# A convolution and attention kernel in fp32: a smaller GpSimd lag while keys are made, and three changes in the closing stage

## The chip, the cores and the metric

The kernel runs on one core of a Trainium2 chip. The metric is the device time of one execution in microseconds (us); lower is better. Engines are named as the profile names them: PE is TensorE (PEld its weight loads), DVE is VectorE, ACT is ScalarE, POOL is GpSimd, SP is SyncE, which issues nearly all DMAs here.

## The reference

The input is four images of 512 channels by 64 x 64 pixels, in fp32. Layer 0 is self-attention over the 4096 pixels of each image with 128 inner channels; layer 1 is an involution (a 7 x 7 filter whose weights are computed for each pixel and for each of 8 groups of 16 channels). Both add their input as a residual. Cut to what matters:

```
q, k, v = wq @ x + bq, wk @ x + bk, wv @ x + bv          # 128 x 4096 per image
attn    = softmax(q^T k)                                 # 4096 x 4096
x       = wo @ (v attn^T) + bo + x                       # 512 x 4096

o = relu(s1 * (W1 @ x) + b1)                             # 128 x 4096
w = Ws @ relu(sr * (Wr @ o) + br) + bs                   # 49 weights per pixel and group
i = sum over the 49 taps of w[tap] * o shifted by tap    # zero padding of 3
x = s3 * (W3 @ i) + b3 + x
```

## The kernel before

An image's 4096 pixels are cut into 8 chunks of 512 pixels (the last chunk of the last image into two halves). For each image there are two stages on PE.

**Making keys** (`keys_values`). The chunks are loaded in the order 2 to 7, 1, 0. For each, PE makes the keys `pk` (four matmuls of 512 columns) and the values `pv` (sixteen of 128 columns); ACT copies both to SBUF.

**Attention** (`attention`). For each chunk of queries PE alternates between scores `pss` (128 keys by 512 queries) and output `po`; ACT takes the exponential into `pt`, and DVE adds the tiles up in `pacc` for the denominator. When a chunk is done, a generator `finish_block` normalises it (`blocks`, `pl`, `rls`, `spread`, `on`), multiplies by Wo (`pwo`, four tiles, each evicted by DVE with the residual, line L513), makes `o1` by W1 (`p1`; the profile calls it `p`), turns it to pixels on partitions (`pp`, `o1t`), writes it to a padded image `pix` in DRAM, and makes the input of the per-pixel weights (`pr`, `red`).

**The involution** (`involution`) runs beside both stages in units of 4 rows of the image, 16 units an image, two units a chunk. Pixels lie on the partitions. `ring` holds 12 rows of the padded image, each with its 7 horizontal shifts, loaded by `pump` from `pix`. `weights` makes `pw`, the 392 weights of each pixel, on PE. A unit is a list of `ops`, 14 to 21 of them: an op is one horizontal shift x and n vertical shifts (n = 4 or 3, or parts of these when the ring wraps around). DVE multiplies the ring rows by the weights (L339), into `acc` for the first op and into one of four buffers `prod` for the others, and POOL adds the product to `acc` (L363). At the end of a unit POOL adds the four parts of `acc` together (L374), `turn_unit` turns the sum to channels on partitions (`pa`, `accT`), and `close_chunk` multiplies a chunk by W3 (`py`, four tiles, each evicted by DVE with scale and residual, L417) and issues the output DMA.

Everything is recorded in one order by a planner. `pe` is its estimate of PE's time, `free["dve"]` and `free["pool"]` its estimates of when the queues of DVE and POOL run empty. `chores` is called between PE's steps and takes one step of `finishing`, one of `closing`, and some of `taps` (the involution). An op of the involution is held back while these estimates are too far ahead of `pe`:

```
while not tail and (
    pe < max(begin, landed)
    or free["dve"] > pe + (4.5 if b == B - 1 else 3.5)
    or free["pool"] > pe + 7.5
):
    yield "wait"
```

When attention of the last image is done, `tail` is set and three queues are emptied in turn: `finishing`, `closing`, `taps`. In this closing stage, some 80 us, the products of odd ops are added by PE and not by POOL: a matmul with the identity `ident` as stationary operand and the product as moving operand adds them into the PSUM tile `accp` (two of the four rows side by side). At the end of such a unit ACT copies `accp` to `accs`, and `turn_unit` turns and adds the four parts of `acc` and the two of `accs` in one group of matmuls with `ident` moving.

`judge` looks whether all reciprocals of the denominators `rls` lie in a safe range (three DVE operations over 128 x 512), sums that over partitions by a small matmul `pn` and writes `verdict`, which decides at the very end whether a slower general path is run; with these inputs it is not.

PSUM tiles with the tag "mm" (`pq`, `pl`, `spread`, `pwo`, `p1`, `pp`, `pr`, `pa`, `py`, `pn`) share two buffers, in turn. All matmuls made by the helper `mm` have line L208.

Of the kernel before, what the change touches and what calls it, by code (L numbers as in the profile page):

```python
# [15 lines left out]
P = 128  # L16
# [53 lines left out]
ROW_US, X_US, PIX_US, LAND_US = 2.2, 3.8, 1.5, 3.0  # L70
HOP_US = 0.8
STEP_US = 1.0
PIECE = 3
TB = 32
WARM = 8
# [5 lines left out]
def fast_path(  # L81
# [65 lines left out]
    pe = 0.0  # L147
    due, seen = 0.0, 0.0
    free = {"dve": 0.0, "pool": 0.0, "dma": 0.0}
    tail = []  # L150
    reds, sums_c = {}, {}
    written = {}
    landing = {}
    low, load = 0, 0

    def until(us):
# [121 lines left out]
    def judge():  # L278
        ok = const.tile([P, B * N // TB], F32, name="ok")
        tc.keep_in_program_order(nc.vector.tensor_scalar(ok, rls, SAFE[0], None, ALU.is_ge))  # L280
        nc.vector.scalar_tensor_tensor(ok, rls, SAFE[1], ok, ALU.is_le, ALU.mult)
        okr = const.tile([P, 1], F32, name="okr")
        nc.vector.tensor_reduce(okr, ok, AX.X, ALU.min)
        pn = ps.tile([1, 1], F32, tag="mm", name="pn")
        nc.tensor.matmul(pn, lhsT=okr, rhs=ones[:, :1], start=True, stop=True)
        nc.vector.tensor_scalar(verdict, pn, P - 0.5, None, ALU.is_lt)


    def involution():
        nonlocal low, due  # L290
        while True:
            while not units:
                yield "none"
            b, u = units.pop(0)
            acc = work2.tile([P, NT, 4, P], F32, tag="acc", name=f"acc_{b}_{u}")
            yield from until(free["dve"] + 0.3)
            pw = early.pop((b, u), None) or weights(b, u)
            begin = pe + 0.5
            accp, ops = None, []
            base = b * STEP + u * UR  # L300
            for dy0, n in DYS:

                at = (base + dy0) % RING
                whole = at + n + NT < RING + 1
                pieces = [(dy0, n)] if whole else [(dy0, 2), (dy0 + 2, n - 2)]
                ops += [(x, dy, k) for x in range(K) for dy, k in pieces]
            for o, (x, dy, n) in enumerate(ops):
                if o and dy >= DYS[1][0] > ops[o - 1][1]:
                    low = base + UR
                    pump()  # L310
                    if tail and units:
                        early[units[0]] = weights(*units[0])
                rows = [(base + dy + t * 2) % RING for t in range(NT)]
                while base + dy + n + NT > load:
                    yield "wait"
                landed = max(landing[base + dy + i] for i in range(n + NT))
                while not tail and (
                    pe < max(begin, landed)
                    or free["dve"] > pe + (4.5 if b == B - 1 else 3.5)
                    or free["pool"] > pe + 7.5  # L320
                ):
                    yield "wait"
                free["pool"] = max(free["pool"], takes("dve", DVE_TAPS[0] + DVE_TAPS[1] * n))
                takes("pool", POOL_TAPS[0] + POOL_TAPS[1] * n)
                due -= n
                d0 = dy - DYS[dy >= DYS[1][0]][0]
                first = x == 0 and dy < DYS[1][0]
                prod, p0 = acc, d0
                if not first:
                    prod, p0 = prods.tile(  # L330
                        [P, NT, 4, P], F32, tag="prod", name=f"prod_{b}_{u}_{o}"
                    ), 0
                col = (x * K + dy) * G
                lines = ring[:, rows[0] : rows[0] + n, x, :]
                image = bass.AP(
                    tensor=lines.tensor, offset=lines.offset,
                    ap=[lines.ap[0], [(rows[1] - rows[0]) * K * P, NT], [K * P, n], [1, P]],
                )
                nc.vector.tensor_tensor(  # L339
                    prod[:, :, p0 : p0 + n, :].rearrange("p t d (g c) -> p t d g c", g=G),  # L340
                    image.rearrange("p t d (g c) -> p t d g c", g=G),
                    pw[:, :, col : col + n * G].unsqueeze(3)
                    .broadcast_to([P, NT, n * G, GC])
                    .rearrange("p t (d g) c -> p t d g c", d=n),
                    ALU.mult,
                )
                if first:
                    pass
                elif tail and o % 2 and (accp is not None or n > 1):

                    begin_sum = accp is None
                    if begin_sum:
                        accp = ps1.tile(
                            [P, NT, 2, P], F32, tag=("po", "acc")[u % 2], name=f"accp_{b}_{u}"
                        )
                    for d in range(0, n, 2):
                        k = min(2, n - d)
                        mm(
                            accp[:, :, :k, :], ident, prod[:, :, d : d + k, :],
                            begin_sum and d == 0, o + 2 >= len(ops) and d + 2 >= n,  # L360
                        )
                else:
                    nc.gpsimd.tensor_tensor(  # L363
                        acc[:, :, d0 : d0 + n, :], acc[:, :, d0 : d0 + n, :], prod[:, :, :n, :],
                        ALU.add,
                    )
                yield
            low = max(low, (b + 1) * STEP if u == NU - 1 else base + UR)
            pump()
            if (b, u) == (B - 1, NU - 1):  # L370
                judge()
            if accp is None:
                for n in (2, 1):
                    nc.gpsimd.tensor_tensor(  # L374
                        acc[:, :, :n, :], acc[:, :, :n, :], acc[:, :, n : 2 * n, :], ALU.add
                    )
            closing.append(turn_unit(b, u, acc, accp, takes("pool", POOL_OP * 1.5)))


    def turn_unit(b, u, acc, accp, done):  # L380
        c, k = divmod(u, 2)
        yield from until(done + 2.0)
        for _ in range(7 if tail else 0):
            yield
        last = (b, c) == (B - 1, NCH - 1)
        if last or k == 0:
            sums_c[b, c] = work1.tile([P, CH], F32, tag="accT", name=f"accT_{b}_{c}")
        pa = ps.tile([P, NT, P], F32, tag="mm", name=f"pa_{b}_{u}")
        if accp is None:
            for t in range(NT):  # L390
                nc.tensor.transpose(pa[:, t, :], acc[:, t, 0, :], ident)
            pe_us(0.25)
        else:

            accs = work1.tile([P, CH // P, P], F32, tag="o1t", name=f"accs_{b}_{u}")
            nc.scalar.copy(accs, accp.rearrange("p t d c -> p (t d) c"))
            for t in range(NT):
                parts = [acc[:, t, d, :] for d in range(4)] + [accs[:, 2 * t + d, :] for d in range(2)]
                for i, part in enumerate(parts):
                    mm(pa[:, t, :], part, ident, i == 0, i == len(parts) - 1)  # L400
        n = NT * P
        nc.scalar.copy(sums_c[b, c][:, k * n : (k + 1) * n], pa.rearrange("p t c -> p (t c)"))
        yield
        if last:
            closing.append(close_chunk(b, c, k * n, n, sums_c.pop((b, c))))
        elif k:
            closing.append(close_chunk(b, c, 0, CH, sums_c.pop((b, c))))


    def close_chunk(b, c, off, n, acc):  # L410
        xt = xs[b, c][:, :, off : off + n]
        yield
        for t in range(CT):
            py = ps.tile([P, CH], F32, tag="mm", name=f"py_{b}_{c}_{off}_{t}")[:, :n]
            mm(py, w_slice(O_W3, t), acc[:, off : off + n])
            takes("dve", DVE_OP * n / CH)
            nc.vector.scalar_tensor_tensor(  # L417
                xt[:, t, :], py, v1(V_S3 + t), xt[:, t, :], ALU.mult, ALU.add
            )
            if n < CH:  # L420
                nc.sync.dma_start(out_r[b, :, t, c * CH + off : c * CH + off + n], xt[:, t, :])
            for _ in range(2):
                yield
        takes("dma", X_US)
        if n == CH:
            nc.sync.dma_start(out_r[b, :, :, c * CH + off : c * CH + off + n], xt)
# [208 lines left out]

    taps = [involution()]
    for b in range(B):
        kv = keys_values(b)
        if b == 0:

            pb = ps.tile([P, CT], F32, tag="mm", name="pb")
# [412 lines left out]
```

## Time and profile before

| | |
|---|---|
| time, median of 3 runs | 2645.77 us (2645.48 to 2646.93) |
| the profiled execution | 2645.35 us, of which its span is 2643.6 us |
| matmuls on PE | 7478 recorded passes, busy 99% of the span |
| DVE, POOL, ACT | busy 70%, 69%, 33% of the span |
| stages of the span | keys of image 0 to about 128 us; keys of images 1, 2, 3 from about 620, 1265, 1910 us, each some 80 us; the closing stage from about 2560 us |

A busy share is an average over stages of different kinds, and PE's ends are modelled from a pipeline, so 99% does not say that PE is at its peak. Every fp32 matmul is recorded as two passes. A line such as `L339 DVE TENSOR_TENSOR prod<-ring,pw 128x768` gives source line, engine, operation, the tile written and those read, and the shape; brackets at its end give the engine's idle time before it and what ended it. Names are without numbers: `acc` is `acc_b_u` for every image and unit. Products and sums of a unit are counted in the order of its ops, from 0.

### The profile page before, as it was taken

The page shows a single profiled execution, that of the slowest core. Times are in us where ns is not written, and L with a number is a line of the kernel's source. Part 1 is how long each engine was busy: PE and PEld are TensorE (multiplying, and loading weights), DVE is VectorE, ACT ScalarE, POOL GpSimd, SP SyncE. Part 2 cuts the span into 40 slices and gives each one's busy share as a digit, 9 for nine tenths or more (in the row PEclk, how much of TensorE's full clock was granted, in tenths as well). Part 3 has the DMA queues.
Part 4 walks back from the last instruction along what each step waited for, and adds up shares of the span by engine and source line. Part 5 has one row for each costly group of instructions (what it writes and reads, how often), then busy time and mean ns, then how long its engine had stood idle before and what let it go on. Part 6 is the DMA issues. An engine that isn't in the chain of part 4 may idle for free.

```text
span 2643.6 us, 24069 instructions
## 1 busy us (share of the span) xinstructions
PE 2614.5 (99%) x7478; PEld 1254.9 (47%) x7478; DVE 1851.5 (70%) x2602; ACT 870.0 (33%) x1454; POOL 1821.4 (69%) x1197
## 2 busy tenths in 40 slices
PE   9999999999999999999999999999999999999998
PEld 7444444445544444444554444444464444444574
DVE  0437788776575778778566677878847667787887
ACT  1333333332333333333223333333323333333330
POOL 0007788788761788888784377878888467777875
PEclk9999999999999999999999999999999999999999
DMA  6032323325614233332450423333353423222343
GB/s 233 0 74 60 92 66 77 77 57 140 157 35 105 60 92 92 92 82 65 121 143 13 106 60 92 92 92 92 92 142 107 97 60 85 69 62 61 75 90 100
DMA packets 104730, 231.70 MB, mean 88 GB/s; under 512 B 5576, under 2 KB 24464, under 8 KB 104464
## 3 DMA queue, kind: packets, MB, share of 16 engines
q1 hardware_dynamic: 104160, 229.70, 35.2%
q8 instruction: 61, 1.00, 0.2%
q14 instruction: 77, 0.63, 0.1%
q10 hardware_dynamic: 432, 0.36, 0.0%
HBM read 187.28 MB, written 42.77 MB: 87 GB/s over the span
## 4 chain that ended last, share of the span: by engine, by line
PE 91%; POOL 4%; DMA 2%; DVE 2%; issue 1%; ACT 0%; SPq 0%; POOLq 0%; DVEq 0%; ACTq 0%
PE pss L208 32%; PE po L208 32%; POOL acc L363 4%; PE pq L208 4%; PE p L208 4%; PE py L208 4%; PE pwo L208 4%; PE pv L208 3%; PE pk L208 3%; DMA ring<-pix 2%; PE pw L208 2%; DVE prod L339 1%; PE pr L208 1%; PE pp L543 1%; PE accp L208 0%
## 5 line engine op out<-in xcount | busy, mean ns | idle before, releaser
L363 POOL TENSOR_TENSOR acc<-acc,prod 128x768 f32<-128x768 f32 (+3 forms) x1063 | 1699.6, 1619 | 797.5 <-DVE prod L339 694.7
L208 PE MATMUL pss<-q,k 128*128 128x512 f32 (+1 forms) x2112 | 1055.2, 584 | 2.3 <-ACT q L469 2.3
L208 PE MATMUL po<-pt,v 128*128 128x512 f32 (+1 forms) x2112 | 1047.0, 580 | 0.0
L596 ACT ACTIVATE pt<-pss 128x512 f32<-128x512 f32 x1024 | 611.2, 597 | 1219.0 <-PE pss L208 1198.7
L339 DVE TENSOR_TENSOR prod<-ring,pw 128x512 f32<-128x512 f32 (+3 forms) x1092 | 899.9, 849 | 147.6 <-POOL acc L363 93.4
L627 DVE TENSOR_TENSOR pacc<-pacc,pt 128x512 f32<-128x512 f32 x958 | 665.3, 695 | 415.6 <-ACT pt L596 405.9
L208 PEld LDWEIGHTS po<-pt,v 128*128 128x128 f32 x2112 | 398.6, 190 | 477.5 <-issue 458.7
L208 PEld LDWEIGHTS pss<-q,k 128*128 128x128 f32 x2112 | 389.3, 190 | 455.0 <-issue 436.3
L208 PE MATMUL py<-accT,wt 128*128 128x512 f32 (+1 forms) x264 | 133.0, 587 | 13.8 <-DVE x L513 12.7
L417 DVE SCALAR_TENSOR_TENSOR x<-py,vec,x 128x512 f32<-128x512 f32 (+1 forms) x132 | 96.4, 730 | 53.6 <-PE py L208 51.6
L208 PEld LDWEIGHTS pv<-wt,x 128*128 128x128 f32 x1024 | 123.3, 198 | 14.8 <-issue 14.8
L208 PE MATMUL pwo<-on,wt 128*128 128x512 f32 (+1 forms) x264 | 129.2, 582 | 0.0
L374 POOL TENSOR_TENSOR acc<-acc 128x512 f32<-128x512 f32 x120 | 119.7, 997 | 9.4
L208 PE MATMUL pv<-wt,x 128*128 128x128 f32 x1024 | 126.0, 282 | 0.0
L339 DVE TENSOR_TENSOR acc<-ring,pw 128x1024 f32<-128x1024 f32 (+1 forms) x84 | 79.4, 964 | 62.4 <-PE pw L208 60.6
L531 ACT ACTIVATE x<-x,vec 128x512 f32<-128x512 f32 (+1 forms) x132 | 92.9, 706 | 81.5 <-PE p L208 76.3
L208 PE MATMUL p<-x,wt 128*128 128x512 f32 (+1 forms) x264 | 119.2, 579 | 0.0
L208 PE MATMUL pk<-x,wt 128*128 128x512 f32 x256 | 117.3, 597 | 0.0
L208 PE MATMUL pq<-x,wt 128*128 128x512 f32 (+1 forms) x264 | 115.6, 580 | 0.0
L513 DVE SCALAR_TENSOR_TENSOR x<-pwo,bo,x 128x512 f32<-128x512 f32 (+1 forms) x132 | 96.4, 733 | 23.6 <-PE pwo L208 20.4
L208 PEld LDWEIGHTS py<-accT,wt 128*128 128x128 f32 x264 | 49.5, 191 | 72.9 <-issue 43.3
L208 PEld LDWEIGHTS pq<-x,wt 128*128 128x128 f32 x264 | 49.7, 190 | 58.8 <-issue 52.7
(57 smaller groups left out, 747.7 us busy)
## 6 DMA issues: line engine op xcount, KB each, us to landing
x<-x_dram SPq DMA_DIRECT2D x55, 1024.0 KB, 5.5
ring<-pix SPq DMA_DIRECT2D x74, 448.0 KB, 10.4
ring<-pix SPq DMA_DIRECT2D x24, 1344.0 KB, 15.8
out_dram<-x SPq DMA_DIRECT2D x31, 1024.0 KB, 4.2
ring<-pix SPq DMA_DIRECT2D x24, 896.0 KB, 13.6
ring<-pix SPq DMA_DIRECT2D x30, 672.0 KB, 10.9
ring<-pix SPq DMA_DIRECT2D x6, 2240.0 KB, 21.0
pix<-o1t SPq DMA_DIRECT2D x62, 128.0 KB, 2.5
```

Source lines behind the costliest of these rows:

```text
L208: return nc.tensor.matmul(o, lhsT=lhsT, rhs=rhs, start=start, stop=stop)
L339: nc.vector.tensor_tensor(prod[:, :, p0 : p0 + n, :].rearrange("p t d (g c) -> p t d g c", g=G), image.rearrange("p t d (g c) -> p t d g c ...
L363: nc.gpsimd.tensor_tensor(acc[:, :, d0 : d0 + n, :], acc[:, :, d0 : d0 + n, :], prod[:, :, :n, :], ALU.add,)
L374: nc.gpsimd.tensor_tensor(acc[:, :, :n, :], acc[:, :, :n, :], acc[:, :, n : 2 * n, :], ALU.add)
L417: nc.vector.scalar_tensor_tensor(xt[:, t, :], py, v1(V_S3 + t), xt[:, t, :], ALU.mult, ALU.add)
L513: nc.vector.scalar_tensor_tensor(xt[:, t, :], pw, bo[:, t : t + 1], xt[:, t, :], ALU.add, ALU.add)
L531: nc.scalar.activation(xt[:, t, :], xt[:, t, :], AF.Identity, bias=v1(V_B3 + t))
L543: nc.tensor.transpose(pp[:, t, :], o1[:, t * P : (t + 1) * P], ident)
L596: nc.scalar.activation(pt, pss, AF.Exp)
L627: nc.vector.tensor_tensor(paccs[k], paccs[k], pt, ALU.add)
```

## The change

- While keys are made, an op of the involution is held back when the estimate of POOL's queue is more than 4.0 us ahead of PE's time, not 7.5 (`POOL_LAG`, `lag`). In attention the bound stays at 7.5.
- In the closing stage PE adds the products of odd ops turned: each 128 x 128 block of the product is the stationary operand and `ident` the moving one, and all blocks are added into `pa`, which is now taken at the unit's first such product, under the tags "po" and "acc" instead of "mm". `accp`, `accs` and ACT's copy between them are gone; `turn_unit` adds only the four parts of `acc` into the same tile.
- In the closing stage the tiles of whole chunks (two tiles of chunk 5, the four of chunk 6) leave PSUM through ACT, which scales them into a buffer `y` of the pool "pt", and POOL adds `y` to the residual `xt`. Halves of the last chunk stay with DVE.
- `judge` is split: the matmul `pn` and the verdict are now recorded by `tell`, after the copy of the last unit's turn.

```diff
--- before.py
+++ after.py
@@ -70,6 +70,7 @@
 ROW_US, X_US, PIX_US, LAND_US = 2.2, 3.8, 1.5, 3.0
 HOP_US = 0.8
 STEP_US = 1.0
+POOL_LAG = 4.0, 7.5
 PIECE = 3
 TB = 32
 WARM = 8
@@ -147,10 +148,12 @@
     pe = 0.0
     due, seen = 0.0, 0.0
     free = {"dve": 0.0, "pool": 0.0, "dma": 0.0}
+    safe = []
     tail = []
     reds, sums_c = {}, {}
     written = {}
     landing = {}
+    lag = 0.0
     low, load = 0, 0
 
     def until(us):
@@ -281,8 +284,11 @@
         nc.vector.scalar_tensor_tensor(ok, rls, SAFE[1], ok, ALU.is_le, ALU.mult)
         okr = const.tile([P, 1], F32, name="okr")
         nc.vector.tensor_reduce(okr, ok, AX.X, ALU.min)
+        safe.append(okr)
+
+    def tell():
         pn = ps.tile([1, 1], F32, tag="mm", name="pn")
-        nc.tensor.matmul(pn, lhsT=okr, rhs=ones[:, :1], start=True, stop=True)
+        nc.tensor.matmul(pn, lhsT=safe[0], rhs=ones[:, :1], start=True, stop=True)
         nc.vector.tensor_scalar(verdict, pn, P - 0.5, None, ALU.is_lt)
 
 
@@ -296,7 +302,7 @@
             yield from until(free["dve"] + 0.3)
             pw = early.pop((b, u), None) or weights(b, u)
             begin = pe + 0.5
-            accp, ops = None, []
+            pa, ops = None, []
             base = b * STEP + u * UR
             for dy0, n in DYS:
 
@@ -317,7 +323,7 @@
                 while not tail and (
                     pe < max(begin, landed)
                     or free["dve"] > pe + (4.5 if b == B - 1 else 3.5)
-                    or free["pool"] > pe + 7.5
+                    or free["pool"] > pe + lag
                 ):
                     yield "wait"
                 free["pool"] = max(free["pool"], takes("dve", DVE_TAPS[0] + DVE_TAPS[1] * n))
@@ -346,19 +352,17 @@
                 )
                 if first:
                     pass
-                elif tail and o % 2 and (accp is not None or n > 1):
-
-                    begin_sum = accp is None
-                    if begin_sum:
-                        accp = ps1.tile(
-                            [P, NT, 2, P], F32, tag=("po", "acc")[u % 2], name=f"accp_{b}_{u}"
-                        )
-                    for d in range(0, n, 2):
-                        k = min(2, n - d)
-                        mm(
-                            accp[:, :, :k, :], ident, prod[:, :, d : d + k, :],
-                            begin_sum and d == 0, o + 2 >= len(ops) and d + 2 >= n,
-                        )
+                elif tail and o % 2:
+
+                    begun = pa is not None
+                    if not begun:
+                        pa = ps1.tile([P, NT, P], F32, tag=("po", "acc")[u % 2], name=f"pa_{b}_{u}")
+                    for t in range(NT):
+                        for d in range(n):
+                            mm(
+                                pa[:, t, :], prod[:, t, d, :], ident,
+                                not begun and t == d == 0, False,
+                            )
                 else:
                     nc.gpsimd.tensor_tensor(
                         acc[:, :, d0 : d0 + n, :], acc[:, :, d0 : d0 + n, :], prod[:, :, :n, :],
@@ -369,15 +373,15 @@
             pump()
             if (b, u) == (B - 1, NU - 1):
                 judge()
-            if accp is None:
+            if pa is None:
                 for n in (2, 1):
                     nc.gpsimd.tensor_tensor(
                         acc[:, :, :n, :], acc[:, :, :n, :], acc[:, :, n : 2 * n, :], ALU.add
                     )
-            closing.append(turn_unit(b, u, acc, accp, takes("pool", POOL_OP * 1.5)))
-
-
-    def turn_unit(b, u, acc, accp, done):
+            closing.append(turn_unit(b, u, acc, pa, takes("pool", POOL_OP * 1.5)))
+
+
+    def turn_unit(b, u, acc, pa, done):
         c, k = divmod(u, 2)
         yield from until(done + 2.0)
         for _ in range(7 if tail else 0):
@@ -385,21 +389,22 @@
         last = (b, c) == (B - 1, NCH - 1)
         if last or k == 0:
             sums_c[b, c] = work1.tile([P, CH], F32, tag="accT", name=f"accT_{b}_{c}")
-        pa = ps.tile([P, NT, P], F32, tag="mm", name=f"pa_{b}_{u}")
-        if accp is None:
+        if pa is None:
+            pa = ps.tile([P, NT, P], F32, tag="mm", name=f"pa_{b}_{u}")
             for t in range(NT):
                 nc.tensor.transpose(pa[:, t, :], acc[:, t, 0, :], ident)
             pe_us(0.25)
         else:
 
-            accs = work1.tile([P, CH // P, P], F32, tag="o1t", name=f"accs_{b}_{u}")
-            nc.scalar.copy(accs, accp.rearrange("p t d c -> p (t d) c"))
             for t in range(NT):
-                parts = [acc[:, t, d, :] for d in range(4)] + [accs[:, 2 * t + d, :] for d in range(2)]
-                for i, part in enumerate(parts):
-                    mm(pa[:, t, :], part, ident, i == 0, i == len(parts) - 1)
+                for d in range(4):
+                    mm(
+                        pa[:, t, :], acc[:, t, d, :], ident, False, t == NT - 1 and d == 3
+                    )
         n = NT * P
         nc.scalar.copy(sums_c[b, c][:, k * n : (k + 1) * n], pa.rearrange("p t c -> p (t c)"))
+        if (b, u) == (B - 1, NU - 1):
+            tell()
         yield
         if last:
             closing.append(close_chunk(b, c, k * n, n, sums_c.pop((b, c))))
@@ -414,9 +419,15 @@
             py = ps.tile([P, CH], F32, tag="mm", name=f"py_{b}_{c}_{off}_{t}")[:, :n]
             mm(py, w_slice(O_W3, t), acc[:, off : off + n])
             takes("dve", DVE_OP * n / CH)
-            nc.vector.scalar_tensor_tensor(
-                xt[:, t, :], py, v1(V_S3 + t), xt[:, t, :], ALU.mult, ALU.add
-            )
+            if tail and n == CH:
+
+                y = ptpool.tile([P, CH], F32, tag="pt", name=f"y_{b}_{c}_{t}")
+                nc.scalar.activation(y, py, AF.Identity, scale=v1(V_S3 + t))
+                nc.gpsimd.tensor_tensor(xt[:, t, :], xt[:, t, :], y, ALU.add)
+            else:
+                nc.vector.scalar_tensor_tensor(
+                    xt[:, t, :], py, v1(V_S3 + t), xt[:, t, :], ALU.mult, ALU.add
+                )
             if n < CH:
                 nc.sync.dma_start(out_r[b, :, t, c * CH + off : c * CH + off + n], xt[:, t, :])
             for _ in range(2):
@@ -635,7 +646,9 @@
 
     taps = [involution()]
     for b in range(B):
+        lag = POOL_LAG[0]
         kv = keys_values(b)
+        lag = POOL_LAG[1]
         if b == 0:
 
             pb = ps.tile([P, CT], F32, tag="mm", name="pb")
```

## The prediction

> **What bounds the kernel now.** I read the page's busy shares first. TensorE (PE) is busy 99% of the span, VectorE (DVE) 70%, GpSimd (POOL) 69%.
>
> ```profile
> PE 2614.5 (99%) x7478; PEld 1254.9 (47%) x7478; DVE 1851.5 (70%) x2602; ACT 870.0 (33%) x1454; POOL 1821.4 (69%) x1197
> ```
>
> So a gain can only come from PE's few idle stretches, from PE work removed, or from the last 80 us, where there are no scores left to compute. The waits of PE over the whole span say where it idles ("us in total, times, longest"):
>
> ```profile
> PE py L208 <- DVE x L513: 12.7, 3, 4.5
> PE accp L208 <- DVE prod L339: 2.4, 1, 2.4
> ...
> PE pa L208 <- POOL acc L363: 1.9, 1, 1.9
> PE pn L285 <- DVE okr L283: 1.3, 1, 1.3
> ```
>
> The first row is one stall in each of the three stages where keys of images 1 to 3 are made (3.95, 4.55 and 4.22 us); the others lie in the tail. The timelines of PE and DVE around the first stall:
>
> ```profile
> 646.97 3.60 PE L208 MATMUL pk<-x,wt 128*128 128x512 f32 x8
> 654.52 1.30 PE L208 MATMUL py<-accT,wt 128*128 128x512 f32 x2 [3.95 <-DVE x L513]
> 655.61 5.24 PE L208 MATMUL pv<-wt,x 128*128 128x128 f32 x32
> ```
> ```profile
> 646.12 0.95 DVE L339 TENSOR_TENSOR prod<-ring,pw 128x768 f32<-128x768 f32 x1 [1.48 <-POOL acc L363]
> 648.54 0.95 DVE L339 TENSOR_TENSOR prod<-ring,pw 128x768 f32<-128x768 f32 x1 [1.47 <-POOL acc L363]
> 650.97 0.95 DVE L339 TENSOR_TENSOR prod<-ring,pw 128x768 f32<-128x768 f32 x1 [1.47 <-POOL acc L363]
> 652.85 0.95 DVE L339 TENSOR_TENSOR prod<-ring,pw 128x768 f32<-128x768 f32 x1 [0.93 <-POOL acc L363]
> 653.72 0.75 DVE L513 SCALAR_TENSOR_TENSOR x<-pwo,bo,x 128x512 f32<-128x512 f32 x1
> ```
>
> Products wait for POOL (four `prods` buffers, POOL back to back), and the eviction of the fourth `pwo` is queued on DVE behind products 7 to 11 of unit 12. The second `py` of chunk 5 needs that `pwo`'s PSUM buffer (two under tag "mm"), so PE stands. Afterwards PE is slow too: 32 `pv` passes take 5.24 us there, 3.7 elsewhere. The windows view shows why (the last columns are granted clock, DMA share and GB/s):
>
> ```profile
> 650.00:655.00 5.00, 1.05 (x3) 0.30 (x2) 3.10 (x4) 0.69 (x1) 4.76 (x4) 1.00 0.02 6
> 655.00:660.00 5.00, 5.00 (x28) 4.57 (x27) 2.60 (x4) 0.00 (x0) 4.84 (x3) 0.66 0.00 0
> ```
>
> In the tail (2560 us on) the groups by form give the prices, and the chain of waits gives the end:
>
> ```profile
> L363 POOL TENSOR_TENSOR acc<-acc,prod 128x512 f32<-128x512 f32 x6 | 7.6, 1274 | 0.4
> L417 DVE SCALAR_TENSOR_TENSOR x<-py,vec,x 128x512 f32<-128x512 f32 x8 | 5.9, 742 | 0.9 <-PE py L208 0.9
> L208 PE MATMUL pa<-ident,accs 128*128 128x128 f32 x32 | 5.2, 275 | 0.0
> ```
> ```profile
> 2630.27 0.70 DVE okr L283
> ...
> 2631.01 0.19 PE pn L285 x2
> 2631.20 0.63 PE py L208 x2
> 2631.82 2.69 PE pa L208 x24
> ...
> 2634.59 0.38 ACT accT L402
> ```
>
> The last turn of unit 15 stands behind a matmul that waits for the safety check on DVE.
>
> **What the Trainium skill says.** "TensorE: Matmul & The Clock Gate", section "What's actually happening": the PE clock is halved after an idle window of about 3.4 us, and the windows run freely. The trace agrees: 0.66 over 5 us is one 3.41 us window at half. Of the windows with PE idle, those idle for 55% or more were mostly followed by a slow one (one of 59% was not), those of 40% or less never; I use 2 us of idleness as the limit. The same page, "Step-by-step": matmuls stay in program order, weight loads are pulled ahead. The trace agrees: everything behind the waiting `py` stood, and `pa` passes start 0.111 us apart, though a weight load is recorded at 0.19. "GPSIMD Engine Reference", "Specifications": no PSUM access; hence the copy by ScalarE (ACT) ahead of the new GpSimd sum. "SBUF — State Buffer", "SBUF: two separate sides": DVE and GpSimd share a port pair under an exclusive lock. No run here isolates that; the 1274 ns row was taken beside DVE work, so the lock, where it acts, is in it.
>
> **Part 1: the smaller lag (4.0 for 7.5) in the key stages.** In the built order only unit 11 and 12 products move. On DVE the normalising steps of chunk 7 pass two products (14 to 18 of unit 11 stood ahead of the reciprocal, now 14 to 16), and the fourth `pwo` eviction stands behind product 9 of unit 12, no longer 11. The second `py`'s eviction stays behind product 13. On PE `pw` of unit 12 goes behind the first `pwo`, `pw` of unit 13 behind `pp` and `pr`, and unit 12's turn half a `pv` group later. No instruction is added, and SP's order is unchanged. Working for image 1:
>
> - `pw` now ends at 634.60 (PE: `pwo` at 632.81, 0.86; `pw` 0.85 and its end), so product 0 of unit 12 starts at 634.65, product 1 ends at 637.00 and its sum starts at 637.14, where it was 636.40: POOL is 0.74 later from here on, back to back as before.
> - Product 9 needs the buffer of product 5, whose sum ended at 648.51: now 649.25. Product 0.95, eviction 0.75, less overlap: the `pwo` is free at 650.89. PE is at the `py` at 650.57 and waits 0.36, where it was 3.95.
> - Full clock now: `py` 0.86, `pv` 3.57, half of `p` 1.72; PE is at the third `py` at 657.08. It needs the second one evicted, behind product 13, which needs sum 9 (656.60, now 657.34): evicted at 658.99. **A new wait of 1.95 us takes the place of the old one**; the third `py` starts at 659.03, before at 662.41. Gain 3.38.
> - Image 2: DVE and POOL have the same times plus 645.01: 1304.04 against 1307.86, gain 3.82. Image 3 (plus 1289.88): 1948.91 against 1952.26, gain 3.35. **Sum 10.55.**
>
> What follows on PE has no wait before `pss <- q` (0.78, stays). What could be late next is DMA, saturated from 675 to 705. It is issued in SP's order behind the output of chunk 5, which follows the fourth `py`'s eviction, so it moves up by the same 3 us; POOL then idles (DVE waits 7.9 us twice for `ring` landings), so no sum is in the way. Bounds per stage: 5.6 if the new wait vanishes, 1.7 if it costs a slow window.
>
> **Part 2: products turned on PE.** A product of n rows was 2n x 128 columns against `ident`; now 2n matmuls of 128 columns. 320 passes at 0.111 against 0.107 (0.429 per 512): +1.3 us, where PE waits anyway. Gone: four `accs` copies (0.59 each on ACT, with PE behind them) and 16 matmuls, 32 passes at 0.111: 3.5 us.
>
> **Part 3: the residual of whole chunks** (two tiles of chunk 5, four of chunk 6). DVE loses 6 x 0.66 (start to start) = 4.0. ACT gains 6 x 0.7, the L531 row (it idles over 80% there). POOL gains 6 x 1.27 = 7.6, at 2575 to 2581 and 2603 to 2616. POOL's waits for products in the tail are 14.3 us, 3.8 of them in the first place, about 4 in the second; there products 18 and 20 of unit 14 will wait for POOL (1.1 and 1.5). Behind the add of chunk 5 on SP stand eight `ring` loads: 1.3 later, and landing over 4 us before use. Walking each engine's built order with these durations, the last product of unit 15 ends at 2627.5, before at 2628.1: the two sides nearly cancel.
>
> **Part 4: the end.** Before, from the end of that product to the last eviction: 2638.09 - 2628.14 = 9.95. Now POOL's last sum ends 1.55 after it, eight turns take 1.78, copy 0.47 with its waits, the four `py` and evictions 3.1 as before: 6.9. The check is beside this path. 3.05 saved. Tail in all 3.5; 1.5 to 5.5 with a slow window more or fewer.
>
> **Sum:** 10.55 + 3.5 = 14.05. The profiled execution took 2645.35 (span 2643.6), so 2631.3; the median shown is 0.4 above it: **2631.7**.
>
> **Rivals.**
> - *The new waits trip the clock.* 1.95 us is at the limit, and wherever a window holds nearly all of it, 1.7 us are lost. For it: 1.89 us sufficed in the tail. Against: 2.0 us in one window at 1940 did not. In all three stages: 2631.7 + 5.1 = 2636.8. Chance 0.18.
> - *POOL makes the tail.* If the sums cost half as much again, or meet the port lock, 6 x 0.65 more, mostly on the path, and the end saves nothing: tail 0 to +2. 2635 to 2638. Against: the 1274 ns row. Chance 0.12.
> - *The wait only moves*: product 13 later than worked out, so the third `py` stands 3 us and goes cold; with a small tail gain within 0.2%, about 2643. Chance 0.06.
> - *Slower: PE bound by weight loads in the tail.* If each turned pass paid its 0.19 us load in the open, 320 x 0.19 = 61 us, less about 10 of PE idleness and 14 gained: 2682. It decides from 0.075 us per pass on. Against: the 0.111 spacing of `pa`. Chance 0.03.
> - *The forecast*: 0.61; its own range 2628.5 to 2635.
>
> **How the numbers follow.** About 0.2% (5.3 us) can be told from no change. Forecast and the first two rivals are beyond that: faster 0.91, same 0.06, slower 0.03. The range: below, the new waits half as long and a tail gain of 5 give 2627; above, the first rival with a tail gain of 2 gives 2638.5.
>
> **What would show it.** Right: the `py <- DVE x L513` row near 1.5 us in total, a row of `py` waiting for its own eviction of about 2 us, three times; 32 `pv` passes at 3.7 us; clock 1.00 in the key stages; no `pn` ahead of the last turn. Wrong: clock below 0.9 there, POOL sums over 1.5 us per 512, `pa` passes over 0.15 us apart, or the third `py` less than 2 us earlier.

## The result and the profile after

| | before | after |
|---|---|---|
| median of 6 runs, us | 2645.70 | 2636.31 (2634.15 to 2636.87) |
| ratio, 95% interval | | 0.9963 (0.9951 to 0.9976) |
| profiled execution, us (span) | 2645.35 (2643.6) | 2636.84 (2634.9) |
| from PE's stop ahead of the first tail product to the end of the span | 79.0 | 82.3 |

The change gains 9.4 us where 14.05 were forecast. The two profiled executions lie 8.6 us apart in their spans, and their traces show where. Ahead of the first product of the tail PE stands for 2.42 us in both kernels; it reaches this stop at 2552.61, before at 2564.55. So **11.9 us are gained ahead of the tail. The tail itself is 3.3 us longer, where it was to be 3.5 shorter.**

Waits of PE over the whole span of after ("us in total, times, longest"):

```profile
PE pa L211 <- DVE prod L345: 9.2, 6, 3.6
PE py L211 <- DVE x L428: 5.1, 3, 1.7
...
PE py L211 <- DVE x L524: 1.1, 3, 0.6
```

The 12.7 us of `py <- DVE x L513` (now L524) are down to 1.1. A row of 5.1, `py` waiting for the eviction of a `py` (L428), has taken part of their place: three waits of 1.7. The first row is new: 9.2 us of waiting for products, all in the tail, where before 2.4 stood.

Timeline of PE around the first key stage of after, and the windows view of it (us, busy time of PE, PEld, DVE, ACT, POOL, then granted clock, DMA share, GB/s):

```profile
651.12 1.13 PE L211 MATMUL py<-accT,wt 128*128 128x512 f32 x2 [0.57 <-DVE x L524]
652.08 3.73 PE L211 MATMUL pv<-wt,x 128*128 128x128 f32 x32
655.65 1.88 PE L211 MATMUL p<-x,wt 128*128 128x512 f32 x4
659.23 1.12 PE L211 MATMUL py<-accT,wt 128*128 128x512 f32 x2 [1.69 <-DVE x L428]
```
```profile
650.00:655.00 5.00, 4.43 (x31) 3.40 (x30) 3.63 (x5) 0.69 (x1) 4.84 (x3) 1.00 0.01 2
655.00:660.00 5.00, 3.31 (x14) 1.72 (x13) 2.57 (x3) 2.03 (x3) 4.76 (x4) 1.00 0.60 178
```

The 32 `pv` passes take 3.73 us instead of 5.24 and the clock is 1.00. The third `py` starts at 659.23 (worked out: 659.03).

Now the tail. Timelines of DVE and of POOL at the end of unit 14, by form:

```profile
2596.50 1.82 DVE L345 TENSOR_TENSOR prod<-ring,pw 128x768 f32<-128x768 f32 x2 [1.07 <-POOL acc L367]
2599.50 0.95 DVE L345 TENSOR_TENSOR prod<-ring,pw 128x768 f32<-128x768 f32 x1 [1.18 <-POOL acc L367]
2602.49 0.95 DVE L345 TENSOR_TENSOR prod<-ring,pw 128x768 f32<-128x768 f32 x1 [2.04 <-POOL acc L367]
```
```profile
2593.42 1.28 POOL L426 TENSOR_TENSOR x<-x,y 128x512 f32<-128x512 f32 x1
2594.65 1.82 POOL L367 TENSOR_TENSOR acc<-acc,prod 128x768 f32<-128x768 f32 x1
2596.42 1.28 POOL L426 TENSOR_TENSOR x<-x,y 128x512 f32<-128x512 f32 x1
2597.64 1.82 POOL L367 TENSOR_TENSOR acc<-acc,prod 128x768 f32<-128x768 f32 x1
2599.40 1.28 POOL L426 TENSOR_TENSOR x<-x,y 128x512 f32<-128x512 f32 x1
2600.64 1.82 POOL L367 TENSOR_TENSOR acc<-acc,prod 128x768 f32<-128x768 f32 x1
```

POOL is without a pause: residual, sum, residual, sum. The three DVE lines are products 17 and 18, 19, and 20 of unit 14. Product 17 starts when the first of these sums (product 14) has ended, at 2596.46; product 19 behind the second (product 16, 2599.46); product 20 behind the third (product 18, 2602.46). So each waits for the buffer of a product only two or three back. The program as built agrees: product 17 is given the buffer of product 14, product 19 that of 16, product 20 that of 18, whereas in unit 12 of image 1, a key stage, every product from 5 on has the buffer of the fourth one before it. In the same stretch of before, DVE ran without a wait, the residual (L417) included:

```profile
2606.26 0.74 DVE L417 SCALAR_TENSOR_TENSOR x<-py,vec,x 128x512 f32<-128x512 f32 x1
2606.93 2.67 DVE L339 TENSOR_TENSOR prod<-ring,pw 128x768 f32<-128x768 f32 x3
2609.52 0.74 DVE L417 SCALAR_TENSOR_TENSOR x<-py,vec,x 128x512 f32<-128x512 f32 x1
```

The chain that ended last shows what the waits of after do, and the timeline of PE the pause:

```profile
2599.40 1.28 POOL x L426
2600.69 1.78 POOL acc L367
2602.46 0.02 issue
2602.49 0.95 DVE prod L345
2603.44 1.13 DVE acc L345
2604.57 1.14 DVE prod L345
2605.72 0.04 issue
2605.76 12.59 PE pa L211 x88
```
```profile
2605.76 3.78 PE L211 MATMUL pa<-ident,prod 128*128 128x128 f32 x16 [3.65 <-DVE prod L345]
```

The chain goes through residual and sum on POOL, product 20, the first two products of unit 15, and then PE. PE had stood for 3.65 us by then (from 2602.11), and the clock was at half from 2604.20 to 2611.03. PE is on the chain from here on nearly to the end.

### The profile page after: what moved, and what is told of

Same layout as the page of the kernel before. It is cut to its first block, busy times and chain, and to the rows that moved or that the text cites. A ratio compares the mean times of both kernels' runs of the same rounds, so it can differ in the third digit from the quotient of the medians.

```text
span 2634.9 us, 24465 instructions
## 1 busy us (share of the span) xinstructions
PE 2607.6 (99%) x7676; PEld 1268.8 (48%) x7676; DVE 1847.8 (70%) x2596; ACT 871.9 (33%) x1456; POOL 1829.0 (69%) x1203
## 4 chain that ended last, share of the span: by engine, by line
PE 94%; POOL 4%; DVE 1%; issue 1%; ACT 0%; POOLq 0%; DVEq 0%; ACTq 0%
PE pss L211 34%; PE po L211 33%; PE pq L211 4%; PE pwo L211 4%; PE p L211 4%; PE py L211 4%; PE pk L211 3%; POOL acc L367 3%; PE pv L211 3%; PE pw L211 2%; DVE prod L345 1%; PE pa L211 1%; PE pr L211 1%; PE pp L554 1%; PE pa L395 0%
## 5 line engine op out<-in xcount | busy, mean ns | idle before, releaser
L524 DVE SCALAR_TENSOR_TENSOR x<-pwo,bo,x 128x512 f32<-128x512 f32 (+1 forms) x132 | 96.6, 734 | 38.8 <-PE pwo L211 35.5
L428 DVE SCALAR_TENSOR_TENSOR x<-py,vec,x 128x512 f32<-128x512 f32 (+1 forms) x126 | 92.1, 731 | 38.4 <-PE py L211 36.5
## 6 DMA issues: line engine op xcount, KB each, us to landing
ring<-pix SPq DMA_DIRECT2D x30, 672.0 KB, 10.9
```

The lines of the kernel that those rows point to most:

```text
L428: nc.vector.scalar_tensor_tensor(xt[:, t, :], py, v1(V_S3 + t), xt[:, t, :], ALU.mult, ALU.add)
L524: nc.vector.scalar_tensor_tensor(xt[:, t, :], pw, bo[:, t : t + 1], xt[:, t, :], ALU.add, ALU.add)
```

## The experiments

All ratios are to the kernel before in the same set of runs. A difference of medians of about 1 us is the least that these runs tell. Where two versions of different sets are compared, as all are with after, their times are subtracted as they stand; the kernel before took 2644.76 to 2645.70 in the five sets, so such a difference is uncertain by another 1 us.

**1. The lag alone**, in the kernel before (the comment is added here):

```diff
-                    or free["pool"] > pe + 7.5
+                    or free["pool"] > pe + lag          # 4.0 in keys_values, else 7.5
```

> The kernel before with the smaller lag in the key stages and nothing else. If the lag gains what the trace after shows (TensorE 11.9 us ahead at its stop before the tail) and the tail is then the old one, the ratio to before is 1 - 11.9/2645.7 = 0.9955, 2633.8 us, faster than the whole change (2636.3). Rival, the lead is eaten by the old tail too (a tail that waits for a landing or has a slow window more): 2636 or more, and the loss of 3.3 us in the tail is not the new tail's doing.

Measured: 2631.86, ratio 0.9954 (0.9940 to 0.9968); 12.9 us gained, 3.5 more than after gained on its own before (4.5 if the times are subtracted). PE's stop before the tail is at 2552.34, as in after, and the old tail is 77.0 long. (It is 2 us shorter than in before because a pause of PE of 1.9 us was followed by half clock there, and is not here.)

**2. The three edits of the tail alone**, in the kernel after:

```diff
-POOL_LAG = 4.0, 7.5
+POOL_LAG = 7.5, 7.5
```

> The kernel after with the old lag of 7.5 everywhere, so the three edits of the tail alone. If the tail of after is longer by 3.3 us for its own reasons, 2649.0 (ratio 1.0012). Rival, the tail was only unlucky in where its pauses fall against the clock windows, which the 12 us of lead shifted: 2639 to 2645, at or below before.

Measured: 2648.20, ratio 1.0014 (1.0007 to 1.0020): 3.4 us lost. PE's wait for products in the tail is again 9.2 us, longest 3.7. So the loss is there without the lead too, and is not an accident of where the lead put the tail's pauses.

**3. The residual back on DVE**, in the kernel after:

```diff
-            if tail and n == CH:
+            if False:
```

> The kernel after with the residual of whole chunks back on VectorE (one instruction per tile); turned products, the check behind the last turn and the lag stay. Theory, GpSimd's residual additions hold back the sums, and with them the product buffers and then TensorE: without them the tail is 5 to 7 us shorter, 2629 to 2631.5. Rival, the turned products cost it: no more than 1 us away from after, 2635.3 to 2637.3. Rival, VectorE is now the bound of the tail and gains nothing from being given the work back: 2633 to 2636.

Measured: 2629.95, ratio 0.9946 (0.9932 to 0.9959). Moving the residual cost 6.4 us (5.4 if each is counted from the before of its own set). Waits of PE in this kernel:

```profile
PE py L211 <- DVE x L428: 5.1, 3, 1.7
PE pa L211 <- DVE prod L345: 3.2, 4, 2.4
...
PE pa L211 <- POOL acc L367: 1.2, 1, 1.2
```

The key stages' row is the same as in after; the row for products has gone from 9.2 to 3.2, and 2.4 of that is the stop before the first product, which every version has. On the chain that ended last, PE goes on earlier than at 2605.76:

```profile
2602.26 3.84 PE pa L211 x32
```

The two tails, 82.3 and 75.7 us, divide thus. Counted from the stop, PE goes on after 53.15 us in after and after 49.58 here: 3.6. From there to the last eviction it takes 22.4 us in after and 20.5 here: 1.8; half clock covers the first 5.3 of them in after and none of them here. Another 1.2 lie behind the last eviction.

**4. The sums as before, the residual on ACT and POOL**: the kernel after with `accp`, `accs` and the old `turn_unit`.

> The kernel after with the sums of the tail's products as before (two rows per matmul, copied by ScalarE, then turned); the residual on ScalarE and GpSimd, the check behind the last turn and the lag stay. Theory, GpSimd's additions cost the tail and the turned products save the copies: slower than after by 1 to 4 us, 2637 to 2640. Rival, the turned products cost it: 2631 to 2634, faster than after.

Measured: 2637.03, ratio 0.9972 (0.9961 to 0.9982); 0.7 slower than after, which these runs do not tell from nothing. The residual costs as much with the old sums (7.4 us against experiment 5).

**5. The lag, and the check behind the last turn**: sums and residual as before. Of the edit only the call that is new against experiment 1 is shown:

```diff
+        if (b, u) == (B - 1, NU - 1):
+            tell()
```

> The kernel before with the lag and with the check's matmul behind the last turn; sums and residual as before. The kernel with the lag alone took 2631.9, the one with turned products besides 2630.0. If moving the check is what saved it (in the trace of the lag alone TensorE still stands 1.26 us ahead of that matmul), 2630.0 to 2630.8; if the turned products did (four copies and their waits), 2631.5 to 2632.

Measured: 2629.62, ratio 0.9944 (0.9931 to 0.9958). Moving `pn` gains 2.2 us on experiment 1; the turned products, all that experiment 3 has besides, gain nothing (+0.3, within the noise).

**6. Five product buffers**, in the kernel after:

```diff
-    prods = pool("prods", 4)
+    prods = pool("prods", 5)
```

> The kernel after with five product buffers instead of four and nothing else; outside the tail the order on every engine stays. Theory, GpSimd's additions hurt because a product then stands still for the buffer of a sum two or three products back: the fifth buffer takes most of TensorE's 9.2 us of waits for products away, 2630 to 2633. Rival, GpSimd's own time is the bound of the tail: one buffer more only moves the wait, 2635.5 to 2637.

Measured: 2623.66, ratio 0.9921 (0.9908 to 0.9935), 12.7 better than after. The tail fell by 5.8 us, which alone would have given 2630.5, as the theory had it. The other 7.0 lie ahead of the tail and were not expected: the three waits for L428 fell from 5.1 to 1.3 us together and those for L524 went, since a product in the key stages then takes the buffer of five products back. With a wait of 0.5 elsewhere these are 5.4 of the 7.0. Waits of DVE in the tail, first of before, then of after, then of this kernel:

```profile
DVE prod L339 <- POOL acc L363: 2.4, 5, 0.9
```
```profile
DVE prod L345 <- POOL acc L367: 10.9, 13, 2.0
```
```profile
DVE prod L345 <- POOL acc L367: 8.0, 10, 1.8
```

DVE still waits for POOL 8.0 us, though with one buffer more PE's wait for products is 6.1 us in all instead of 9.2. Its pause ahead of unit 15 fell from 3.65 to 1.81, and no half clock followed it.

**7. ScalarE scales, DVE adds**, in the kernel after:

```diff
-                nc.gpsimd.tensor_tensor(xt[:, t, :], xt[:, t, :], y, ALU.add)
+                nc.vector.tensor_tensor(xt[:, t, :], xt[:, t, :], y, ALU.add)
```

> The kernel after with the six residual additions on VectorE instead of GpSimd; ScalarE still copies and scales ahead of them. Theory, it is the 6 x 1.28 us on GpSimd that cost: 2629.5 to 2631.5, as with the residual all on VectorE (2630.0). Rival, the detour over ScalarE (one hop more before a PSUM buffer or x is free) costs: 2633 to 2637.

Measured: 2633.07, ratio 0.9953 (0.9939 to 0.9967): 3.2 better than after, but 3.1 short of the residual in one DVE instruction. The five executions fall into two groups, 2630.3 and 2630.6, and 2633.1 to 2634.2: in the first nearly all of the loss is gone, in the second about half of it stayed. The profiled one is of the second group. The timelines of DVE and POOL show a cost that no theory had named:

```profile
2592.99 1.72 DVE L426 TENSOR_TENSOR x<-x,y 128x512 f32<-128x512 f32 x1
2594.64 0.94 DVE L345 TENSOR_TENSOR prod<-ring,pw 128x768 f32<-128x768 f32 x1
2595.50 0.68 DVE L426 TENSOR_TENSOR x<-x,y 128x512 f32<-128x512 f32 x1
2596.10 2.74 DVE L345 TENSOR_TENSOR prod<-ring,pw 128x768 f32<-128x768 f32 x3
2598.76 1.65 DVE L426 TENSOR_TENSOR x<-x,y 128x512 f32<-128x512 f32 x1
```
```profile
2592.36 1.81 POOL L367 TENSOR_TENSOR acc<-acc,prod 128x768 f32<-128x768 f32 x1 [0.48 <-DVE prod L345]
2595.72 2.13 POOL L367 TENSOR_TENSOR acc<-acc,prod 128x768 f32<-128x768 f32 x1 [1.56 <-DVE prod L345]
2598.06 1.81 POOL L367 TENSOR_TENSOR acc<-acc,prod 128x768 f32<-128x768 f32 x1 [0.20 <-DVE prod L345]
```

The same DVE addition takes 0.68 or 1.7 us. The long ones began while a POOL sum was running (until 2594.17 and 2599.87) and end 0.55 us after its end. The short one began ahead of a POOL sum, and that sum took 2.13 instead of 1.81. They exclude each other. The other three of the six additions fit: one long one (1.39) ended 0.55 us after a sum's end, and two of 0.68 each stand beside a sum that took 0.32 longer than its like.

The lock alone is not the 3.1 us. The longer additions lie on the chain that ended last, and PE waits longer for the last sum of unit 14, 1.2 us in experiment 3 and here:

```profile
PE pa L211 <- POOL acc L367: 2.8, 1, 2.8
```

Counted from its stop PE goes on 1.5 us later than in experiment 3. Then half clock (2602.59 to 2609.41) makes the same passes up to the check take 19.8 us instead of 16.9. That the executions of the first group lack this half clock is likely (mean granted clock 0.999 in both, 0.998 in the three others), but no trace shows one. The rival, the detour over ScalarE, does not show: no copy `y` is on the chain in the last 40 us of work.

**8. A smaller lag still**, in the kernel of experiment 3:

```diff
-POOL_LAG = 4.0, 7.5
+POOL_LAG = 2.0, 7.5
```

> The kernel after with the residual on VectorE (2630.0) and a lag of 2.0 in the key stages instead of 4.0. Theory, each key stage still has 1.7 us of waiting for a py behind VectorE's products, of which a smaller lag takes two thirds or all: 2625 to 2629. Rival, products put off pile up and are late in the tail or hold a ring load: 2631 to 2640. Rival, the waiting product stands there whatever the lag: 2629.5 to 2630.5.

Measured: 2635.15, ratio 0.9967 (0.9955 to 0.9979), 5.2 worse than experiment 3. Waits of PE, and one of the new ones with DVE beside it:

```profile
PE pss L211 <- ACT pt L607: 6.0, 3, 2.0
...
PE py L211 <- DVE x L428: 2.1, 3, 0.9
```
```profile
708.27 1.22 PE L211 MATMUL pss<-q,k 128*128 128x512 f32 x2 [2.02 <-ACT pt L607]
```
```profile
706.23 0.69 DVE L345 TENSOR_TENSOR prod<-ring,pw 128x512 f32<-128x512 f32 x1 [0.80 <-POOL acc L367]
706.84 0.69 DVE L636 COPY pacc<-pt 128x512 f32<-128x512 f32 x1
```

The time is that of the second expectation, its place is not. The waits for `py` fall from 5.1 to 2.1, but the products put off now stand ahead of `pacc` at the beginning of attention: DVE waits for POOL, `pacc` reads `pt` late, ACT's next `pt` and then PE's scores wait, 2.0 us in each image.

**9. Five buffers, residual on DVE** (experiment 3 with five).

> Five product buffers, lag 4.0, turned products, check behind the last turn, and the residual of whole chunks on VectorE. With the residual on ScalarE and GpSimd this took 2623.7 (7.0 us of its gain on after lay ahead of the tail, 5.8 in it). Theory, GpSimd's additions cost only through the buffers: with five it makes no difference where the residual is added, 2622.5 to 2624.5. Rival, GpSimd's own time still counts, as it did with four (6.3 us): 2617 to 2621.

Measured: 2622.66, ratio 0.9914 (0.9901 to 0.9928). With five buffers moving the residual costs 1.0 us, with four 6.4. The theory is borne out but for that 1.0, which is at the edge of what the runs tell.

**10. Five buffers, lag, check moved, sums and residual as before** (experiment 5 with five).

> The kernel before with the lag, the check behind the last turn and five product buffers; sums and residual as before (2629.6 with four buffers). The gain of 7.0 us ahead of the tail must come here too. Theory, the turned products are worth nothing with VectorE adding the residual: the same as the run with turned products beside it, within 1 us, and 2620 to 2624. Rival, turned products free TensorE from waits for copies once VectorE is no longer held: 2 us or more behind that run.

Measured: 2622.34, ratio 0.9912 (0.9897 to 0.9927): the same as experiment 9. The turned products gain nothing with five buffers either.

**11. Five buffers in the kernel before**, nothing else.

> The kernel before with five product buffers, nothing else (lag 7.5). The product that held the eviction back waits for a sum one place earlier, 2.4 us sooner, so each of the three stalls of 4.0 to 4.6 us shrinks to about 1.7 and no longer costs a window at half clock: 3 x (2.4 + 1.7) = 12 less, 2632 to 2635, as much as the lag gave with four buffers (2631.9). Rival, five buffers let one more product in ahead of the eviction, and the stall stays: 2643 to 2646.

Measured: 2631.29, ratio 0.9951 (0.9938 to 0.9965). The fifth buffer does for the old kernel what the lag does. Its waits of PE show why:

```profile
PE py L208 <- DVE x L513: 6.7, 3, 2.5
```

12.7 us have become 6.7 (2.47, 2.20 and 2.03), and half clock follows only the last of the three. The two cures add up in part: both together, with the check moved, give experiment 10, 9 us below this, of which 2.2 is the check.

**12. Six buffers** (experiment 10 with six).

> The kernel before with the lag, the check behind the last turn and six product buffers (2622.3 with five). If buffers still bind, the remaining waits of py for its eviction in the key stages (1.4 us in three) and the wait of the turn of unit 14 for GpSimd (1.1 us) shrink: 2620 to 2621.5. Rival, with five the products wait for GpSimd or TensorE itself and no longer for a buffer: within 1 us of 2622.3.

Measured: 2620.35, ratio 0.9908 (0.9894 to 0.9922), 24.7 us below before in the same set of runs. **This version beats both kernels**, with the lag and the moved check but neither the turned products nor the moved residual. PE has no wait left for a `py` eviction in the key stages; the wait of unit 14's turn for POOL (1.1) stayed.

## Why the prediction was right, and where its steps were not

The time fell within the range and on the side that had 0.91, but outside the forecast's own range of 2628.5 to 2635: the key stages gained more than worked out, and the tail lost where it was to gain. That it lay within the range is in part luck. The key stages gained 1.4 us too much, which covered a part of the 6.8 that the tail missed, and the upper end of the range had been set for another cause, half clock in the key stages.

- **Part 1, the lag: right, a little low.** Leads per image at `pss <- q`: 3.3, 4.9, 3.8 us (worked out 3.38, 3.82, 3.35); together 12.0 for 10.55. The new waits are 1.7 us each, not 1.95. The replacement of the wait by a shorter one, the recovered clock and the passed products were as worked out. That is experiment 1: 12.9.
- **Rival "the new waits trip the clock": refuted.** Three waits of 1.7 and none followed by half clock, here or in experiments 1, 3, 4, 5 and 7. It was near, though: in experiment 9 the stop ahead of the tail put 1.69 us of idleness into one window of 3.41, and half clock followed.
- **Part 2, turned products: pass price right, gain wrong.** The passes are 0.112 us apart (0.111), which also refutes the rival of weight loads in the open. But of the 3.5 us of the `accs` nothing came out: experiments 3 and 5, and 9 and 10, show no gain. In the trace of experiment 3 unit 15's last product ends 1.6 us later than in experiment 5 (1.1 counted from PE's stop), and the way from it to the last eviction is 1.0 shorter. Why the turned sums delay the products was not tried.
- **Part 3, the residual: this is the step that failed.** "Walking each engine's built order with these durations, the last product of unit 15 ends at 2627.5, before at 2628.1: the two sides nearly cancel." Counted from PE's stop, the product ends 67.6 us on, before 63.6: 4.0 later instead of 0.6 earlier. The durations were right: residual additions took 1.28 us (1.27), POOL's busy time rose by 7.6 as worked out. The term that was mis-sized is the waiting: "products 18 and 20 of unit 14 will wait for POOL (1.1 and 1.5)" became products 17, 19 and 20 with 1.07, 1.18 and 2.04, and with the others 10.9 us in 13 waits, before 2.4. Part 1 lets product 9 take the buffer of product 5, and that here only even products, whose sums are POOL's, were to wait fits the same rule of four back. It holds in the key stages, where all sums are POOL's. In the tail sums alternate between PE and POOL, and trace and built program show products waiting for POOL's sum two or three back. So POOL's idle time of 14.3 us was no room for six residual additions: those at the end of unit 14 stood in the loop from sum to product. Experiment 3 puts their price at 6.4. Of the 6.6 between the two traces 3.6 is the longer pause of PE, 1.8 goes with the half clock behind it, and 1.2 lies behind the last eviction. Experiments 6 and 9 show it to be buffers for the most part: 1.0 with five.
- **Part 4, the end: mechanism right, size off.** From the last product to the last eviction 7.95 us, before 9.95; worked out 6.9. In experiment 3, where PE is not behind, it is 7.03. The moved check is worth 2.2 by itself. Another 1.3 us passed between the last eviction and the end of the span in after (6.8, before 5.5, experiment 3 5.6). It is so in the traces of experiments 2 and 4 too (7.2 and 7.1), which also have four buffers and POOL's additions, and in no other (5.0 to 5.9); what it is, is not settled.
- **Rival "POOL makes the tail": right in its number, wrong in its cause.** It gave 2635 to 2638 and named POOL, but from sums that cost half as much again. They did not (1.28 us); POOL's order and the buffers sufficed.

Measured by experiments, then: lag -12.9, check -2.2, turned products +0.3, residual +6.4; the sum is -8.4, and the change measured -9.4. This is no proof that the effects add up: the four are steps from one kernel to the next (before, experiments 1, 5 and 3, after), so they must sum to the change, and the 1.0 between is the difference of the two medians of before.

## What to carry to other kernels

An engine with idle time is not free to take work if its results hand buffers back to the engine that feeds it: count how soon a buffer comes back, not how long the engine is busy, and look in the trace which earlier instruction each wait ends with in that very stage. Which buffer a product gets can be read from the built program. A wait that is caused by too long a queue has two cures, a shorter queue and more buffers; try the buffers first, since here one more was worth as much as the lag, and a lag too small only moved the wait to the next stage. When edits come in a bundle, price them one by one: the bundle's gain here was two good edits less a bad one, and one that did nothing.

## What was not expected of the hardware

A DVE addition with both operands in SBUF and a POOL sum exclude each other for a whole instruction (experiment 7): 1.39 to 1.72 us instead of 0.68, ending 0.55 after the POOL sum, or else POOL's 1.81 becomes 2.13. DVE products with `pw` in PSUM took 0.68 per 128x512, at most 0.69, beside POOL in all kernels. The Trainium skill, "SBUF — State Buffer", section "SBUF: two separate sides", states this: an exclusive lock of the port pair that the two share, taken for the whole instruction by whichever starts first, and for a DVE operation with two SBUF inputs only against GpSimd operations that read SBUF. The trace agrees: the DVE additions that came second end 0.55 us after the sum, the sums that came second are 0.32 longer. The prediction named that lock for POOL's own additions, where no run showed it (1.28 us beside DVE's products).

The clock does not follow the length of a pause alone: in experiment 11 pauses of 2.47 and 2.20 us were not followed by half clock and one of 2.03 was. The starts of half clock lie a whole number of times 3.41 us apart (in before the first two 641.7, which is 188 times); in windows laid on these steps the three pauses left at most 1.72, 1.44 and 2.03 us idle in one window. That is no sharp limit either: 2.01 us in one window of before (from 1938.76) was not followed by half clock, and 1.69 in experiment 9 was. The stop of 2.42 us ahead of the tail is in every kernel; after it half clock lasted 3.41 us in before and after, and 6.83 in experiments 2, 6 and 9.
